# A four-layer graph network on one core: layer 0's sums in one PSUM bank, two quarters side by side, and paired loads of the adjacency matrix

## The chip, the cores and the metric

The kernel runs on one NeuronCore of a Trainium2 chip. The metric is the device time of one execution in microseconds; lower is better. A profile is one further execution, recorded by the hardware profiler, with a time of its own.

## The reference

There are 4096 nodes with 64 features each and a 4096 x 4096 matrix `adj` of zeros and ones, about 0.8% of them ones. Four layers follow each other, each of the form `x = x + layer(relu(layernorm(x)), adj)`. What matters here are the first two.

```python
# layer 0: each row of adj weighs its (up to 100) last neighbours by powers of 1/2
support = input @ weight
rank = jnp.cumsum(mask, axis=1)          # mask = adj != 0
deg = rank[:, -1:]
k = jnp.minimum(deg, 100.0)
pos = rank - (deg - k)
w = mask * jnp.where(pos > 0, 0.5 ** (k - pos), 0.0)
out = w @ support + bias
# layer 1: attention, masked by adj
att = sigmoid((2 + 2 * (qm @ k.T)) / att_scale + att_bias)
support = (adj * att) @ h
out = support / sqrt(abs(inner(support)))
```

Here `h`, `q` and `k` of layer 1 are linear maps of the features with a first component that is made from the others. Layer 2 applies a gated unit to `adj @ x` twice, and layer 3 a hyperbolic mean over `adj`.

## The kernel before

`adj` is held on the chip, transposed, as one byte per element: 64 tiles `A[q][i]` of 128 partitions x 2 x 1024. A *quarter* `q` is 1024 rows of the output, a *block* `b` is 128 neighbours, and a tile holds the two blocks `2i` and `2i+1`. The tiles stay for all four layers.

**Layer 0** (`stream0`, with `post0` behind it) takes the quarters one after another, and in each the 32 blocks from the last to the first. A block is loaded by POOL's queue, with a cast from f32 to bytes in the transfer, 512 KB from `in_adjT`; this load waits for the one eight loads back (`after=loads[-8:-7]`). One block in eight is *staged* instead: SP loads it as f32 into a working tile, POOL casts it (`L1210`), and VectorE tests its values (`test`). Then, for each half `c` of the quarter (512 rows), TensorE counts the ones that come later, with a triangular matrix (`ftri`), into a bank `cnt`; ACT or VectorE turns the counts into weights (`weigh`, `L1233` or `L1235`), reading the count's bytes; TensorE updates the counts with `fupd`, so that the next block can be counted. The weights of two rows share one f32 word, so an instruction of 256 words has 512 weights. Counting, weighing and updating are a loop: the next block of the same half can't be counted before this one has been weighed. `add` then multiplies the block's features `S0` by the weights: the weights are the stationary operand, eight matmuls of 128 x 128 a block, node-major, into two banks `sum`. `post0` reduces them, turns them by four transposes (`turn4`, `L1038`), multiplies by `w0` (`linear4`) and adds to `X[q]`.

**Between the layers** `pre1(q)` makes the keys `kT[q]`, the queries (sent through the DRAM tile `qs` to all partitions) and `S1[q]`. It is a chain of small instructions on VectorE, ACT, TensorE and POOL, whose `root` (`L997`) is a power on POOL, the engine that also issues the loads.

**Layer 1** (`stream1`) takes each quarter and in it pairs of blocks `i` from 0 to 15. For each half `c`, four f32 matmuls of 64 x 64 x 512 make the scores in two banks `sc`, ACT applies a sigmoid (`L1008`), VectorE multiplies by `A` (`L968`), and `add` sums into two banks `acc` with four matmuls of 64 x 64 x 512 for each block; `post1` adds the two banks. A *group* below is such a set of four matmuls: 128 for scores and 128 for sums. Pair `i` needs the keys of quarter `i // 4`.

**Order.** A planner (`Plan`) fixes the order of all engines when the kernel is built. It takes operations by priority and by the costs and limits written into it. Each engine then runs its own list in that order. PSUM has eight banks: places 0 to 3 can be taken in pairs, 4 to 7 are single. `limits` holds how many of a kind may be in use; `anywhere` names the kinds that may take any place; `single` lets at most three of the single banks be held by other kinds than `nw`. So two of `cnt` leave one of these for others.

The values of `adj` not tested in layer 0 are tested later by `later_test` (f32 loads on SP, `L1187` on VectorE, `L1189` and `L1190` on ACT), 36 of them spread over layer 1 and the rest after it. `general_kernel` is a second program for other inputs, which is not entered here.

Of the kernel before, what the change touches and what calls it, by code (L numbers as in the profile page):

```python
# [38 lines left out]
def general_kernel(ctx: ExitStack, tc: tile.TileContext, t: dict, out: bass.AP):  # L39
# [9 lines left out]

    nc = tc.nc  # L50
    adjT = t["adjT"]
    N = adjT.shape[0]
    NB = N // P
    HB = NB // NH
    HN = N // NH
# [161 lines left out]
    def aggregate(m, lhs, weigh, descending, evac, post):  # L217

        pairs = list(range(NB // 2))[::-1] if descending else list(range(NB // 2))
        packed = m == D
        for h in range(NH):
            n_acc = NCH // 2 if packed else NCH
            banks = [accp.tile([P, CW], F32, tag=f"acc{c}", name=f"acc{c}") for c in range(n_acc)]
            if packed:
                accs = [banks[c // 2][(c % 2) * D:(c % 2) * D + D, :] for c in range(NCH)]  # L230
            else:
                accs = [bank[:m, :] for bank in banks]

            def accumulate(i, pair, s, rhs):
                for j in ((1, 0) if descending else (0, 1)):
                    b = 2 * pair + j
                    for c in (2 * s, 2 * s + 1):
                        nc.tensor.matmul(accs[c], lhs(b), rhs(j, c),
                                         start=(i == 0 and j == int(descending)),
                                         stop=(i == NB // 2 - 1 and j == int(not descending)))  # L240

            behind = None
            for i, pair in enumerate(pairs):
                a = adjp.tile([P, 2, HN], F32, tag="a", name="a")
                nc.sync.dma_start(a, adjT[pair * 2 * P:(pair + 1) * 2 * P, h * HN:(h + 1) * HN]
                                  .rearrange("(j p) n -> p j n", p=P))
                for s in range(NCH // 2):
                    rhs = weigh(h, i, pair, s, a)
                    if behind is not None:
                        accumulate(*behind)  # L250
                    behind = (i, pair, s, rhs)
                if h > 0 and i == 1:
                    post(h - 1)
            accumulate(*behind)
            evac(h, accs)
        post(NH - 1)
# [377 lines left out]
class Plan:  # L634
# [61 lines left out]
    def find(self, b):  # L696
# [19 lines left out]
            return (best[1], best[2]) if best else (math.inf, None)  # L716
        if self.psn.get(b.kind, 0) + b.units > self.limits.get(b.kind, 8):
            return math.inf, None
        places = range(0, 4, 2) if b.units == 2 else range(8) if b.kind in self.anywhere else range(4, 8)
        if b.kind != "nw" and self.psn.get("single", 0) >= 3:  # L720
            places = [i for i in places if i < 4]
        best = None
# [178 lines left out]
def fast_kernel(ctx: ExitStack, tc: tile.TileContext, t: dict, out: bass.AP, flag: bass.AP):  # L901
    nc = tc.nc
    adjT = t["adjT"]
    N = adjT.shape[0]
    NB = N // P
    L = Layout()
    V, S_, G_ = nc.vector, nc.scalar, nc.gpsimd
# [5 lines left out]
    dram = ctx.enter_context(tc.tile_pool(name="fdram", bufs=1, space=bass.MemoryType.DRAM))  # L913

    plan = Plan(NSB, {"cnt": 2, "sum": 2, "sc": 4, "acc": 3, "acc2": 3, "acc3": 6, "nw": 4,
                      "w": (24, 16), "g": (5, 6), "stage": (5, 8), "qd": (4, 0), "mx": (4, 0)}, ("sum", "acc3"))

    sb_tiles = [const.tile([P, 2 * CW], F32, name=f"m{i}") for i in range(NSB)]
    st_tiles = [const.tile([P, 16], F32, name=f"s{i}") for i in range(NST)]
# [19 lines left out]
    def sb(units, name):  # L939
        return fresh("sb", units, name)  # L940
# [7 lines left out]
    def bank(kind, units=1):  # L948
        return fresh(kind, units, kind)
# [174 lines left out]
    def a8(q, b):  # L1124
        return A[q][b // 2].part(b % 2)[:, b % 2, :]
# [19 lines left out]

    S0 = {}

    loads = []

    def halves(dst, x, prio, relu=False):  # L1150

# [24 lines left out]

    def staged(q, b):
        n = q * NB + NB - 1 - b
        return n > 8 and n % 8 == 1

    def test(b, q, s, prio, cost):
        i = q * NB + b
# [9 lines left out]

    def later_test(b, q, after, cost):
        s = sb(4, "stage")
        dma(s, View(None, lambda: adjT[b * P:(b + 1) * P, q * 2 * CW:(q + 1) * 2 * CW]), P * 2 * CW * 5, 8.0, after=after)
        return test(b, q, s, 9.0, cost)


    def stream0(q, behind):
        cnt = [bank("cnt") for _ in range(2)]  # L1200
        sums = [bank("sum") for _ in range(2)]
        for b in range(NB)[::-1]:
            a = a8(q, b)
            src = View(None, lambda b=b: adjT[b * P:(b + 1) * P, q * 2 * CW:(q + 1) * 2 * CW])
            if b in behind:
                behind[b](loads[-1:], (q, b + 1))
            if staged(q, b):
                s = sb(4, "stage")
                dma(s, src, P * 2 * CW * 5, 1.0, after=loads[-2:-1])
                plan.op({"POOL": 1.4}, lambda e, a=a, s=s: G_.tensor_copy(a.get().bitcast(U8), s.get(), saturate=False),  # L1210
                        (s,), (a,), 1.0)
                test(b, q, s, 1.9, {"DVE": 1.58})
            else:
                loads.append(dma(a.bits(U8), src, P * 2 * CW * 4, 0.9 if len(loads) < 2 else 1.0, "POOL", after=loads[-8:-7]))
            wts = []
            for c in (0, 1):
                pairs = slice(c * CW // 2, (c + 1) * CW // 2)

                def count(e, c=c, a=a, pairs=pairs, b=b, wt=tri):
                    mm(cnt[c].get()[:, :CW // 2], wt, a.get().bitcast(F16)[:, pairs], False, b == 0)  # L1220

                if b == NB - 1:
                    plan.op({"PE": 0.12}, lambda e, c=c: mm(cnt[c].get()[:, :CW // 2], mean16, half16, True, False),
                            (triv,), (cnt[c],), 1.0, "full")
                plan.op({"PE": 0.112}, count, (a, triv), (cnt[c],), 1.0, "full")
                wt = sb(1, "w").bits(I16)
                wts.append(wt)

                def weigh(e, c=c, wt=wt):
                    o = wt.get().rearrange("p (n k) -> p n k", k=2)  # L1230
                    s = cnt[c].get()[:, :CW // 2].bitcast(I8).rearrange("p (n k) -> p n k", k=4)[:, :, :2]
                    if e == "ACT":
                        S_.activation(o, s, AF.Relu, scale=-128.0)  # L1233
                    else:
                        V.tensor_scalar(o, s, -128.0, 0.0, op0=ALU.mult, op1=ALU.max)  # L1235
                plan.op({"ACT": 0.6, "DVE": 0.69}, weigh, (cnt[c],), (wt,), 0.5)
                if b:
                    plan.op({"PE": 0.112}, lambda e, count=count: count(e, wt=upd), (a, triv), (cnt[c],), 1.0, "full")
            for c in (0, 1):
                def add(e, b=b, c=c, wt=wts[c]):  # L1240
                    s = S0[b // QB].get()[:, b % QB]
                    o = sums[c].get().rearrange("p (k n) -> p k n", k=4)
                    for d in range(4):
                        mm(o[:, d, :].rearrange("p (k d) -> p k d", d=D), wt.get()[:, d * P:(d + 1) * P].bitcast(BF16), s,
                           b == NB - 1 and d == 0, b == 0)
                plan.op({"PE": 0.24}, add, (wts[c], S0[b // QB]), (sums[c],), 2.0, "full")
        return sums

    def post0(q, sums, prio):
        g = nodes("agg")  # L1250
        for c in range(2):
            red(g.part(c)[:, c * CB:(c + 1) * CB, :], sums[c].re("p (b k d) -> p b d k", k=2, d=D), CW, prio)
        fm = sb(2, "aggT")
        copy(fm, turn4(flat(g), prio), prio=prio, scale=W0 / HALF)
        tt(X[q], X[q], blocks(linear4(fm, w("w0"), prio)), ALU.add, prio=prio)
        pre1(q, prio)

# [75 lines left out]

    ends = {}
    scores = []

    def stream1(q):
        qd = []
        for c in range(2):
# [3 lines left out]
                dma(v.part(r)[half, :], View(qS[q].buf, lambda c=c: qS[q].get()[c * D:(c + 1) * D, :]), D * CW * 4, 1.0,  # L1343
                    after=ends.get(("qd", q), ()))
            qd.append(v)
        acc = [bank("acc") for _ in range(2)]
        for i in range(NB // 2):
            gs = []
            for c in range(2):
# [16 lines left out]
            for j in range(2):  # L1366
                def add(e, i=i, j=j, gs=gs):
                    b = 2 * i + j
                    s = S1[b // QB].get()[:, b % QB, :]
                    for r in range(2):  # L1370
                        half = slice(r * D, (r + 1) * D)
                        for c in range(2):
                            mm(acc[r].get()[c * D:(c + 1) * D, :], s[half, :], gs[c].get()[half, j, :], b == 0, b == NB - 1)
                ends[1, q, i] = plan.op({"PE": 0.856}, add, (*gs, S1[(2 * i) // QB]), tuple(acc), 3.1, "corner")
        return acc

    def post1(q, acc, prio):
        a = sb(2, "a")
        fn(a, acc[0], AF.Copy, prio=prio)
        tt(a, a, acc[1], ALU.add, prio=prio)  # L1380
        sup = blocks(turn4(a, prio))
        sq = nodes("sq")
        square(sq, sup, prio=prio)
# [307 lines left out]
    def load_consts(after, behind):  # L1691
        gate(Wv, lambda: W[:1, :1], behind)
        dma(Wv, View(None, lambda: t["consts"][:, :L.at["scales"].stop]), P * L.at["scales"].stop * 4, 0.1, after=after)
        for q in range(NQ):
# [2 lines left out]
        subnormals(3.0)  # L1697

    load_x(3)
    behind = {NB - 2: lambda *a: load_x(2, *a), NB - 5: lambda *a: load_x(1, *a), NB - 9: lambda *a: load_x(0, *a),  # L1700
              NB - 13: load_consts}
    sums = {}
    for q in range(NQ):
        sums[q] = stream0(q, behind if q == 0 else {})
        post0(q, sums[q], 0.9 if q < NQ - 1 else 0.4)
    acc = {}
    for q in range(NQ):
        if q:
# [42 lines left out]
        for o in plan.order(NST):  # L1751
            o.emit(o.on)
    return plan


def pack_consts(given):

    import numpy as np
# [82 lines left out]
```

## Time and profile before

| what | value |
|---|---|
| median of three runs | 688.46 us (687.64 to 690.23) |
| profiled execution, own time | 691.17 us |
| profiled execution, span | 689.3 us |
| TensorE clock granted, mean | 0.976 |
| busy: TensorE, VectorE, ACT, POOL | 622.3, 548.6, 450.6, 167.9 us |
| first and last `ftri` matmul | 6.3 and 202.2 us |
| loads of `adj` on POOL | 113, issued from 1.2 to 182.1 us |
| loads of `adj` on SP | 128 (15 in layer 0) |

The span runs from the first instruction to the last; the execution's own time also has what lies around them. TensorE's busy time is an upper bound for the work that it had, since matmuls are pipelined and their ends are modelled. The stages of the span are layer 0 up to 203 us, layer 1 up to about 440, layer 2 up to about 600, layer 3 up to about 660, and an end without TensorE.

### The profile page before, as it was taken

The page shows a single profiled execution, that of the slowest core. Times are in us where ns is not written, and L with a number is a line of the kernel's source. Part 1 is how long each engine was busy: PE and PEld are TensorE (multiplying, and loading weights), DVE is VectorE, ACT ScalarE, POOL GpSimd, SP SyncE. Part 2 cuts the span into 40 slices and gives each one's busy share as a digit, 9 for nine tenths or more (in the row PEclk, how much of TensorE's full clock was granted, in tenths as well). Part 3 has the DMA queues.
Part 4 walks back from the last instruction along what each step waited for, and adds up shares of the span by engine and source line. Part 5 has one row for each costly group of instructions (what it writes and reads, how often), then busy time and mean ns, then how long its engine had stood idle before and what let it go on. Part 6 is the DMA issues. An engine that isn't in the chain of part 4 may idle for free.

```text
span 689.3 us, 14988 instructions
## 1 busy us (share of the span) xinstructions
PE 622.3 (90%) x6060; PEld 355.2 (52%) x6060; DVE 548.6 (80%) x1030; ACT 450.6 (65%) x680; POOL 167.9 (24%) x188
## 2 busy tenths in 40 slices
PE   4788889899999999999999999999999999999950
PEld 2666668678764443333333333344444444599950
DVE  5675776776768899998987799887988988985585
ACT  3464757577666666676665567645987698984463
POOL 6535564574422200200110010011000022202141
PEclk9899999999999999999999999999999999999995
DMA  9999989989902233422322231369689978420001
GB/s 99 181 251 106 95 66 147 178 73 157 125 17 62 77 93 97 120 62 93 108 57 97 92 112 62 123 220 390 202 264 352 342 250 260 154 63 2 3 31 36
DMA packets 39934, 91.64 MB, mean 133 GB/s; under 512 B 4656, under 2 KB 19632, under 8 KB 39856
## 3 DMA queue, kind: packets, MB, share of 16 engines
q1 hardware_dynamic: 23584, 75.78, 33.1%
q0 software_dynamic: 16272, 14.82, 24.2%
q8 instruction: 49, 0.80, 0.5%
q14 instruction: 29, 0.24, 0.1%
HBM read 130.82 MB, written 2.10 MB: 193 GB/s over the span
## 4 chain that ended last, share of the span: by engine, by line
PE 63%; DVE 16%; DMA 8%; ACT 6%; issue 3%; POOL 3%; SPq 0%; POOLq 0%; ACTq 0%; DVEq 0%
PE p L1029 61%; DVE m L968 4%; DMA A<-in_adjT 3%; ACT m L1008 3%; PE p L1038 3%; DMA m<-in_adjT 3%; DVE m L1235 2%; DVE m L985 2%; POOL s L997 2%; DMA m<-in_x_pm 2%; ACT m L1233 2%; DVE s L990 2%; DVE junk L1187 2%; POOL A L1025 1%; DVE s L968 1%
## 5 line engine op out<-in xcount | busy, mean ns | idle before, releaser
L1029 PE MATMUL p<-m,m 64*64 64x512 f32 (+1 forms) x3012 | 337.8, 476 | 8.5 <-ACT m L1008 3.7
L997 POOL TENSOR_TENSOR s<-s,powers 128x8 f32<-128x8 f32 (+1 forms) x45 | 89.3, 1992 | 461.4 <-DVE s L979 199.4
L1008 ACT ACTIVATE m<-p,fatt_add,fatt_mul 128x1024 f32<-128x1024 f32 x128 | 149.6, 1201 | 77.2 <-PE p L1029 63.6
L1029 PEld LDWEIGHTS <-m 128*128 128x128 bf16 (+1 forms) x2048 | 134.0, 105 | 75.5 <-issue 22.0
L968 DVE TENSOR_TENSOR m<-m,A 128x1024 f32<-128x1024 f32 x128 | 152.8, 1221 | 19.8 <-ACT m L1008 19.4
L1029 PEld LDWEIGHTS p<-m,m 64*64 64x64 f32 (+1 forms) x2040 | 81.0, 132 | 142.4 <-issue 81.8
L1233 ACT ACTIVATE m<-p 128x512 int16<-128x512 int8 x180 | 103.7, 596 | 52.5 <-PE p L1029 47.1
L1187 DVE SCALAR_TENSOR_TENSOR junk<-m 128x1024 uint8<-128x1024 f32 x98 | 119.5, 1220 | 8.2 <-DMA m<-in_adjT 7.3
L1029 PE MATMUL p<-A,m 128*64 128x512 fp8e4 x1024 | 116.4, 381 | 0.0
L1029 PE MATMUL p<-A,fupd 128*128 128x256 f16 x248 | 67.6, 283 | 13.9 <-DVE m L1235 6.0
L1235 DVE TENSOR_SCALAR m<-p 128x512 int16<-128x512 int8 x76 | 52.3, 690 | 30.7 <-PE p L1029 23.3
L1029 PE MATMUL p<-A,ftri 128*128 128x256 f16 x256 | 68.9, 286 | 6.5 <-POOL A L1210 3.8
L1008 ACT ACTIVATE m<-m 128x512 f32<-128x512 f32 (+4 forms) x96 | 53.6, 567 | 30.4 <-DVE m L968 14.6
L1025 POOL DMA_DIRECT2D A<-in_adjT x113 | 61.0, 553 | 39.7 <-DMA A<-in_adjT 38.4
L1029 PE MATMUL p<-m,A 128*128 128x132 f16 x1024 | 61.4, 220 | 1.5 <-ACT m L1008 1.2
L1029 PEld LDWEIGHTS <-A 128*128 128x128 fp8e4 x1024 | 60.1, 96 | 4.0 <-issue 4.0
L990 DVE TENSOR_REDUCE s<-m 128x8 f32<-128x512 f32 (+2 forms) x66 | 43.3, 661 | 9.1 <-DMA m<-in_x_pm 7.1
L1029 PEld LDWEIGHTS <-ftri 128*128 128x128 bf16 x256 | 25.6, 100 | 33.5 <-issue 26.1
L1008 ACT ACTIVATE m<-p 128x512 f32<-128x512 f32 (+4 forms) x40 | 19.2, 491 | 33.4 <-PE p L1029 24.0
L1190 ACT ACTIVATE junk<-m,big 128x1024 uint8<-128x1024 f32 x30 | 34.5, 1149 | 1.0
L1189 ACT ACTIVATE junk<-m 128x1024 uint8<-128x1024 f32 x30 | 31.4, 1047 | 1.7 <-DMA m<-in_adjT 1.5
L1038 PE MATMUL p<-fident,m 128*128 128x128 f32 x160 | 25.8, 284 | 6.8 <-DVE m L968 4.5
(102 smaller groups left out, 429.3 us busy)
## 6 DMA issues: line engine op xcount, KB each, us to landing
m<-in_adjT SPq DMA_DIRECT2D x128, 512.0 KB, 5.7
A<-in_adjT POOLq DMA_DIRECT2D x113, 128.0 KB, 9.9
m<-qs SPq DMA_DIRECT2D x16, 128.0 KB, 4.4
m<-m SPq DMA_DIRECT2D x16, 128.0 KB, 6.9
m<-in_x_pm SPq DMA_DIRECT2D x4, 256.0 KB, 6.6
qs<-m SPq DMA_DIRECT2D x4, 256.0 KB, 5.2
out_x<-m SPq DMA_DIRECT2D x3, 256.0 KB, 2.1
m<-in_consts SPq DMA_DIRECT2D x2, 256.0 KB, 5.2
```

The source lines that it names most:

```text
L968: return plan.op(cost or {"DVE": dve(n)}, lambda e: ENG[e].tensor_tensor(o.get(), a.get(), b.get(), op), (a, b), (o,), prio)
L990: return plan.op({"DVE": dve(n)}, lambda e: V.tensor_reduce(o.get(), a.get(), AX.X, ALU.add), (a,), (o,), prio)
L997: lambda e: G_.tensor_tensor(o.get(), a.get(), POWER[power].get().to_broadcast([P, n]), ALU.pow),
L1008: S_.activation(o.get(), a.get(), func, **k)
L1025: return plan.op({eng: 0.06 if eng == "SP" else 0.55}, lambda e: ENG[e].dma_start(o.get(), a.get()), (a,), (o,), prio, nbytes=nbytes, afte ...
L1029: nc.tensor.matmul(o, lhsT, rhs, start=start, stop=stop, skip_group_check=True)
L1038: nc.tensor.transpose(o[:, j * P:(j + 1) * P], s[:, j * P:(j + 1) * P], ident)
L1187: V.scalar_tensor_tensor(junk, s.get(), 0.0, s.get(), op0=ALU.not_equal, op1=ALU.not_equal, accum_out=odd[:, i:i + 1])
L1189: S_.activation(junk2, s.get(), AF.Exp, scale=-BIG0, accum_out=zeros[:, i:i + 1])
L1190: S_.activation(junk2, s.get(), AF.Exp, bias=big1, scale=BIG1, accum_out=ones_of[:, i:i + 1])
L1233: S_.activation(o, s, AF.Relu, scale=-128.0)
L1235: V.tensor_scalar(o, s, -128.0, 0.0, op0=ALU.mult, op1=ALU.max)
```

## The change

Five edits come together.

1. `adj` lies in DRAM by quarter, pair of blocks, partition, block of the pair and column, so that the two blocks of a tile are one run of 8 KB in each partition. POOL loads a tile at once (1 MB), except a quarter's first two blocks and the partner of a staged block. The waits are for the load six back, and for staged blocks four back.
2. Layer 0's sums take `S0` as the stationary operand, 64 wide, and the weights as the moving one, 512 wide: four matmuls a block, the two halves of the quarter on the two halves of the partitions of one bank. The result is feature-major, and `post0` loses its reductions and its transposes.
3. Quarters 1 and 2 are streamed together, block by block in turn. Each has one bank of counts with 512 words, so one weighing has 1024 weights. Quarters 0 and 3 keep two banks and weighings of 512. All counts are made in 64-wide matmuls.
4. Layer 1's first quarter sums in one bank, with two matmuls of 128 x 64 x 512 a block in place of four of 64 x 64 x 512.
5. `cnt` is put into places 0 and 1, and `sum` no longer into any place. Staged blocks fall on another residue of eight.

```diff
-        places = range(0, 4, 2) if b.units == 2 else range(8) if b.kind in self.anywhere else range(4, 8)
+        places = range(0, 4, 2) if b.units == 2 else range(2) if b.kind == "cnt" else range(8) if b.kind in self.anywhere else range(4, 8)
...
-                      ...}, ("sum", "acc3"))
+                      ...}, ("acc3",))
...
     def staged(q, b):
         n = q * NB + NB - 1 - b
-        return n > 8 and n % 8 == 1
+        return n > 8 and n % 8 == 5
...
-    def stream0(q, behind):
-        cnt = [bank("cnt") for _ in range(2)]
-        sums = [bank("sum") for _ in range(2)]
+    def stream0(qs, behind):
+        cnts = {q: [bank("cnt") for _ in range(2 // len(qs))] for q in qs}
+        sums_ = {q: bank("sum") for q in qs}
         for b in range(NB)[::-1]:
+            for q in qs:
+                block0(q, b, cnts[q], sums_[q], behind)
+        return sums_
+
+    def block0(q, b, cnt, sums, behind):
+        a = a8(q, b)
+        src = View(None, lambda: adjT[q, b // 2, :, b % 2, :])
...
+        if staged(q, b):
+            s = sb(4, "stage")
+            dma(s, src, P * 2 * CW * 5, 1.0, after=loads[-4:-3])
...
+        elif staged(q, b ^ 1) or b // 2 == NB // 2 - 1:
+            loads.append(dma(a.bits(U8), src, P * 2 * CW * 4.6, ..., "POOL", after=loads[-6:-5]))
+        elif b % 2:
+            loads.append(dma(A[q][b // 2].re("p j n -> p (j n)").bits(U8),
+                             View(None, lambda: adjT[q, b // 2].rearrange("p j n -> p (j n)")),
+                             2 * P * 2 * CW * 4.3, 1.0, "POOL", after=loads[-6:-5]))
...
+        parts = len(cnt)
+        wide = CW // parts
+        for c in range(parts):
+            def count(e, c=c, wt=tri):
+                s = a.get().bitcast(F16)
+                for h in (0, 1):
+                    half = slice(h * D, (h + 1) * D)
+                    if parts == 1:
+                        mm(cnt[c].get()[half, :], wt[:, half], s, False, b == 0)
+                    else:
+                        mm(cnt[c].get()[half, :wide]..., wt[:, half], s...[:, c], False, b == 0)
...
         def add(e):
+            for k in (0, 1):
+                for c in (0, 1):
+                    mm(sums.get()[c * D:(c + 1) * D, :].rearrange("p (j n) -> p j n", n=P), s[:, k, :], v[c],
+                       b == NB - 1 and k == 0, b == 0 and k == 1)
+        plan.op({"PE": 0.432}, add, (*wts, S0[b // QB]), (sums,), 2.0, "narrow")
 
     def post0(q, sums, prio):
-        g = nodes("agg")
-        for c in range(2):
-            red(g.part(c)[:, c * CB:(c + 1) * CB, :], sums[c].re("p (b k d) -> p b d k", k=2, d=D), CW, prio)
         fm = sb(2, "aggT")
-        copy(fm, turn4(flat(g), prio), prio=prio, scale=W0 / HALF)
+        copy(fm, sums, prio=prio, scale=W0 / HALF)
...
+    EARLY = 1
+    GROUPS = ((0,), (1, 2), (3,))
     def stream1(q):
...
-        acc = [bank("acc") for _ in range(2)]
+        early = q < EARLY
+        acc = [bank("acc") for _ in range(1 if early else 2)]
...
                     s = S1[b // QB].get()[:, b % QB, :]
+                    if early:
+                        for c in range(2):
+                            mm(acc[0].get()[c * D:(c + 1) * D, :], s, gs[c].get()[:, j, :], b == 0, b == NB - 1)
+                        return
...
-    for q in range(NQ):
-        sums[q] = stream0(q, behind if q == 0 else {})
-        post0(q, sums[q], 0.9 if q < NQ - 1 else 0.4)
+    for qs in GROUPS:
+        sums = stream0(qs, behind)
+        for q in qs:
+            post0(q, sums[q], 0.9 if q < NQ - 1 else 0.4)
...
-        "x": given("x"), "adjT": transposed("adj"),
+        "x": given("x"), "adjT": given("adj").reshape(NQ, 2 * CW, -1, 2, P).transpose(0, 2, 4, 3, 1),
```

## Prediction

> **What bounds the kernel now.** I read the page's slices first, then busy time by stretches, then the chain of waits, then the groups by form.
>
> ```profile
> PE   4788889899999999999999999999999999999950
> ...
> DMA  9999989989902233422322231369689978420001
> ```
>
> Columns are 17.2 us. TensorE is busy nearly everywhere, but up to about 185 us the DMA engines are full too. Layer 0 and layer 1 have different limits.
>
> ```profile
> 6.00:61.00 55.00, 41.28 (x368) 32.26 (x368) 33.51 (x63) 28.72 (x52) 27.79 (x40) 0.91 1.09 176
> ...
> 158.00:203.00 45.00, 41.95 (x445) 34.28 (x442) 32.19 (x61) 32.09 (x59) 18.48 (x22) 1.00 0.78 108
> ...
> 300.00:360.00 60.00, 60.00 (x544) 20.17 (x536) 53.44 (x65) 38.91 (x37) 5.09 (x2) 1.00 0.25 76
> ```
>
> The stretches of 6 to 203 us are the quarters of layer 0: the first `ftri` matmul starts at 6.3, the last at 202.2 (the tile view of `ftri`). From 300 to 360 TensorE has no gap, and 544 records (two per f32 matmul, four matmuls a group) are 68 groups: **0.88 us a group**. Layer 1 is bound by TensorE. Layer 0 is paced by three things close together, as the chain and the queue of POOL show.
>
> ```profile
> 86.21 3.64 POOL A L1025 x7
> 89.84 6.19 issue
> 96.07 3.86 POOL s L997 x2
> ...
> 197.66 1.04 PE p L1029 x12
> 198.72 1.04 PE p L1029 x12
> ```
>
> ```profile
> 54.07 0.53 POOL L1025 DMA_DIRECT2D A<-in_adjT  x1 [0.79 <-DMA A<-in_adjT]
> 55.29 0.53 POOL L1025 DMA_DIRECT2D A<-in_adjT  x1 [0.70 <-DMA A<-in_adjT]
> 56.50 0.53 POOL L1025 DMA_DIRECT2D A<-in_adjT  x1 [0.69 <-DMA A<-in_adjT]
> 57.76 0.53 POOL L1025 DMA_DIRECT2D A<-in_adjT  x1 [0.73 <-DMA A<-in_adjT]
> ```
>
> The second is POOL's timeline. When POOL only loads, it waits for the load eight back and issues one each 1.24 us: 512 KB of `adj` read in 1.24 us is 423 GB/s. **All 128 blocks at that pace are 159 us**, `x` and the constants (1.5 MB) 3.6 us more, the first landing 5 us: a DMA floor of 168 us. The last load is issued at 182.1 and takes some 9 us, so it lands near 191. The 23 us above the floor are holes, of which the chain shows one: seven loads, then POOL stands for 6.2 us before two roots of `pre1`, then works 3.9 us, and issues nothing for 10 us, as long as eight loads in flight last. The stream itself ends 11 us after the last landing. And where blocks come back to back, a block is 12 matmuls in **1.04 us** of TensorE.
>
> **What the Trainium skill says.** "DMA: Bandwidth & Descriptors", Rules for kernel authors, wants 1 MiB or more per DMA; its section Anatomy of one DMA gives 2.0 us plus bytes over 436 GB/s. The trace's 423 GB/s with eight loads of 512 KB in flight is within 3% of that, so size alone can buy little. "TensorEngine Tiling (Array Packing)", Key Properties: column tiles run in parallel, and a change of mode drains TensorE. The layer 2 row below agrees on the first; no row prices the drain. "VectorE: DVE Perf Modes", The TRN2 errata, prices a read of PSUM by ScalarE at 172 + n cycles of 1.2 GHz and by VectorE at 120 + n of 0.96 GHz: 0.57 and 0.66 us for n = 512, where the trace has 0.596 and 0.690.
>
> **The change, part by part.** Prices:
>
> ```profile
> L1029 PE MATMUL p<-A,m 128*64 128x512 fp8e4 x1024 | 116.4, 381 | 0.0
> L1233 ACT ACTIVATE m<-p 128x512 int16<-128x512 int8 x180 | 103.7, 596 | 52.5 <-PE p L1029 47.1 <-DVE m L1235 2.1 <-issue 0.5
> ...
> L1029 PEld LDWEIGHTS <-m 128*64 128x64 f16 x1024 | 55.4, 110 | 62.7 <-issue 16.3
> L1235 DVE TENSOR_SCALAR m<-p 128x512 int16<-128x512 int8 x76 | 52.3, 690 | 30.7 <-PE p L1029 23.3 <-ACT m L1233 6.7
> ```
>
> *TensorE in layer 0.* A narrow 512-wide matmul of two side by side costs 116.4/1024 = 0.114 us, its weight load (55.4/1024 = 0.054) hidden. The sums become 4 of these, 0.455 us a block, for 8 of 128 x 128. Counts become 8 narrow of 256 in quarters 0 and 3, 4 narrow of 512 in quarters 1 and 2; by streamed columns both are 0.455. No row shows a 256-wide narrow one. Bounds for a block: 0.91 with all loads hidden; with every count's load exposed, 0.91 + 8 x 0.054 = 1.34 (quarters 0 and 3) and 1.13 (1 and 2). I take 0.95, because layer 3's 128-wide loads and 132-wide matmuls run 1024 in 61.4 us, 0.06 each, so loads hide behind matmuls of similar length. Then 128 x (1.04 - 0.95) = 11.5 us of TensorE fall away. The built order has 18 of layer 1's 256 groups ahead of layer 0's last matmul; now it is 3 (24 records in the window to 202.5), because `single` lets three of the four single banks be held at once: 2 for `cnt` leave 1, and `acc` asks for 2. With `cnt` in banks 0 and 1, sums (2) and one `acc` fit. These 15 cost 15 x 0.88 = 13.2 us inside layer 0, about what is freed there. **After layer 0 they are 13 us less.**
>
> *Weighing and posts.* 64 instructions of 1024 replace 128 of 512. With the page's slope on the measured rows (an estimate) they take 1.02 on ACT and 1.22 on DVE: some 128 x 0.62 - 64 x 1.1 = 9 us less over both, with a longer link of the loop count, weigh, update, but two quarters advance per link. At 0.25 + 1.1 + 0.25 and hops of 0.3 a link is some 1.9 to 2.3 us for two blocks, under the 2.48 that their loads take. `post0` loses 8 reductions (5.5 us of DVE) and 4 turns (2.6 us by 25.8/160 a transpose); only quarter 3's share, 2 x 0.69 + 4 x 0.16, about 2 us, leads a chain that is waited for. The first `post1` loses one 0.69 add, under cover of layer 1. I count these at nothing; without cover they give 2 us.
>
> *Loads.* 45 pair loads and 23 single ones replace 113, so POOL issues 45 times less, 25 us at 0.55, which are mostly waits now. Six may fly, on average 10 blocks (113/68 each) for 8: 12.4 us against 10. Thus a stop like that at 89.8 is covered by 2.5 us more. A pair is available when its second half lands: up to 1.24 us later, which matters for the first pair only, since later blocks lead by 10 us. Behind a waiting load on POOL stand the casts of staged blocks and the roots of `pre1`, whose DVE steps wait for them; these are as many as before. SP has the same 15 staged loads, let go by the load four back; two tests of layer 1 slip into layer 0, 2.5 us of DMA. 8 KB rows for 4 KB: the trace has none; no gain up to 3% of 159 us, or a loss of as much, 5 us both ways. I take no change of rate, and that **two thirds to three quarters of the 34 us between the floor and 202 stay**: holes go from 23 to 13, the lag at the end from 11 to 3. Layer 0 ends at 184, 18 us sooner.
>
> *What is late next.* Quarters 1 and 2 end together, so `pre1` of quarter 1 starts 32 blocks later, and only key blocks 0 to 3 (16 groups, and two scores more) can go ahead. After layer 0 the next wait is for quarter 3's keys: now they come at 238 (`qs` issued at 238.2), 35 us after layer 0, with 30 groups, 26 us, and pre-ops between. The new order has 30 there too, so that cover holds. Everything from layer 2 on has the same order.
>
> *Sum.* The profiled execution's own time is 691.2 (span 689.3); the median of the runs is 688.5, 2.7 lower. 691.2 - 18 - 13.2 = 660.0 for a profile, **657 as a median**.
>
> **Rivals.**
> - *The loads gain nothing.* POOL still stops at roots, the DMA queue has the same holes. Then layer 0 ends at 202 and 13 us remain: 675. For it: POOL waited 44.8 us for DVE in layer 0; against: more blocks in flight.
> - *The floor is reached.* Last landing at 168, end at 171: 31 + 13 us, 644. Against it: three roots of `pre1` for each of two quarters now fall together.
> - *Narrow weight loads are exposed (slower).* Each matmul of the counts has its own 64-wide load, 64 x 8 + 64 x 4 = 768 of them. At the upper bound a block is 1.24 on average: 158 us for 133 now, plus 29 for the rest (transposes, `W` products, presets, groups) and 13 for the new groups: 200. With half of the present 202 - 133 - 29 = 40 us of waits layer 0 ends at 220: 18 later, 13 back, 693. It decides once the exposed loads eat the 31 us of the forecast, 0.04 us for each of 768, three quarters of a load. Against it are the layer 2 and 3 rows; for it, that none of them is 256 wide and that `pre1` and scores change the mode in between.
> - *No difference:* the 15 groups lengthen layer 0 by what they save later, with the loads unchanged: 688.
>
> **Chances.** Forecast 0.52, floor 0.15, loads gain nothing 0.17, exposed loads 0.11, no difference 0.05. So faster by over 0.5% (3.4 us, about what a measurement of this kernel tells from no change) 0.84, within it 0.05, slower 0.11. The range goes from the floor, 643, to 686, which leaves out the slower case and little else; the forecast alone is 649 to 668.
>
> **What would show it.** Right: last narrow count matmul of layer 0 at 176 to 192, 18 layer 1 groups before it, POOL's pair loads 2.5 us apart where it only loads, then 0.88 us a group with TensorE full up to layer 2. A block of 12 or 8 matmuls back to back in 0.95 us. Wrong: pairs further apart than 2.6 us; 1.2 us or more for a block; or TensorE idle some 10 us before the scores of quarter 3's keys, which would mean that the groups moved were the cover of `pre1`.

## The result, and the profile after

The changed kernel is slower. Its median is **773.97 us** (771.04 to 777.09, four runs) against 689.35 us for the kernel before beside it: a ratio of 1.123, 95% interval 1.1176 to 1.1284. The profiled execution took 773.04 us, its span is 771.2 us. One execution each of e1 and e21 below ran much longer at a lower granted clock, and their medians leave it out.

Three lines of the slices on the changed kernel's page, a column now 19.3 us; the second is the granted TensorE clock in tenths:

```profile
PE   4656667685777778999999999999999999999950
...
PEclk9766699789999979999999999999999999999995
DMA  9998054899706402131322322424977997720000
```

TensorE is not full before the seventeenth column, and the DMA engines have long stretches with little or nothing. Four stretches of the changed kernel follow; the prediction shows three of the same windows of the kernel before (columns: start and end, length, busy time of TensorE, weight loads, VectorE, ACT, POOL, then clock, DMA share and GB/s):

```profile
6.00:61.00 55.00, 33.31 (x244) 19.85 (x244) 26.46 (x49) 19.77 (x35) 21.28 (x28) 0.77 1.07 172
61.00:158.00 97.00, 65.86 (x439) 36.84 (x437) 40.28 (x70) 35.96 (x48) 20.38 (x26) 0.80 0.54 54
158.00:203.00 45.00, 33.72 (x238) 13.77 (x236) 19.95 (x18) 20.42 (x20) 10.79 (x17) 0.99 0.96 152
300.00:360.00 60.00, 58.98 (x388) 19.54 (x388) 52.14 (x76) 37.46 (x40) 9.36 (x5) 1.00 0.25 78
```

In the first of these, 55 us long, TensorE begins 244 matmuls where it began 368, and no compute engine is full; the DMA engines still are (1.07), and fall to 0.54 in the second. The last row is layer 1, nearly as full as before. The tile view of `ftri` puts the end of layer 0 at **296.8 us** (202.2 before): 94.6 us later. What follows takes 771.2 - 296.8 = 474.4 us, where it took 689.3 - 202.2 = 487.1: 12.7 us less. So the loss lies in layer 0 alone.

The chain of waits of the changed kernel, in quarter 0 (start, duration, what), shows how a block goes:

```profile
83.06 0.61 ACT m L1257
83.66 0.02 issue
83.69 0.70 DVE m L1259
84.39 0.04 issue
84.43 1.07 PE p L1029 x12
85.50 0.02 issue
85.53 0.61 ACT m L1257
86.13 0.02 issue
86.16 0.70 DVE m L1259
86.86 0.04 issue
86.90 1.08 PE p L1029 x8
```

One block takes from 84.43 to 86.90, 2.47 us, and the two weighings in it, on two engines and of two different banks, never overlap: VectorE starts 0.03 us after ACT ends. In the chain of before, two blocks start 1.06 us apart (197.66 and 198.72). The waits say the same. First the kernel before, then the changed kernel (engine and line, what it waited for, total us, times, longest), each over its layer 0:

```profile
DVE m L1235 <- ACT m L1233: 6.7, 8, 1.2
...
PE p L1029 <- DVE m L1235: 6.0, 11, 2.0
...
PE p L1029 <- ACT m L1233: 4.1, 10, 0.6
```

```profile
DVE m L1259 <- ACT m L1257: 56.8, 35, 3.9
...
PE p L1029 <- DVE m L1259: 42.9, 45, 2.0
PE p L1029 <- ACT m L1257: 40.8, 62, 1.2
```

A weighing on VectorE that waits for one on ACT has no reason in the arithmetic: they read different counts and write different weights. At 85.50 TensorE has made both counts of the block (the last four of its twelve matmuls are `ftri`, two for each half); VectorE, which only reads its own half, still waits for ACT, which only reads the other. These are waits on semaphores: in the trace the instruction of VectorE at 86.16 waits on the semaphore that ACT's instructions raise, and on none of TensorE's.

**Theory.** Edit 5 put the two `cnt` into places 0 and 1, which are the two halves of one two-bank PSUM tile, `p0`. Instructions of different engines on that tile are put in order, whichever half they touch, so the two loops of a block become one. Before, each `cnt` had a tile of one bank. **Rivals:** narrow weight loads that don't hide; the lower clock; the queues of POOL and SP with pair loads; the order of quarters 1 and 2.

### The profile page after: what moved, and what is told of

Its sections match the earlier page's. It is cut to its first block, busy times and chain, and to the rows that moved or that the text cites. A ratio compares the mean times of both kernels' runs of the same rounds, so it can differ in the third digit from the quotient of the medians.

```text
span 771.2 us, 14016 instructions
## 1 busy us (share of the span) xinstructions
PE 644.4 (84%) x5664; PEld 320.1 (42%) x5664; DVE 539.0 (70%) x1004; ACT 444.3 (58%) x633; POOL 139.8 (18%) x143
## 4 chain that ended last, share of the span: by engine, by line
PE 61%; DVE 15%; ACT 13%; DMA 6%; issue 3%; POOL 1%; ACTq 0%; SPq 0%; POOLq 0%; DVEq 0%
PE p L1029 59%; ACT m L1257 9%; DVE m L1259 6%; DVE m L968 4%; ACT m L1008 2%; PE p L1038 2%; DMA m<-in_adjT 2%; DVE junk L1187 2%; DVE m L985 1%; DMA m<-in_x_pm 1%; POOL s L997 1%; DVE s L990 1%; DMA qs<-m 1%; DMA m<-qs 1%; DMA A<-in_adjT 1%
## 5 line engine op out<-in xcount | busy, mean ns | idle before, releaser
L1029 PE MATMUL p<-m,m 64*64 64x512 f32 (+2 forms) x2420 | 334.8, 565 | 5.7 <-DVE m L1718 3.2
L1257 ACT ACTIVATE m<-p 128x512 int16<-128x512 int8 (+1 forms) x130 | 94.8, 734 | 148.2 <-PE p L1029 140.4
L1029 PEld LDWEIGHTS p<-m,m 64*64 64x64 f32 (+1 forms) x1952 | 76.1, 132 | 150.7 <-issue 87.6
L1259 DVE TENSOR_SCALAR m<-p 128x512 int16<-128x512 int8 (+1 forms) x62 | 54.6, 880 | 113.0 <-ACT m L1257 56.8
L1029 PEld LDWEIGHTS <-m 128*64 128x64 f16 x1536 | 93.5, 115 | 77.3 <-issue 18.2
L1029 PE MATMUL p<-A,fupd 128*64 128x256 f16 (+1 forms) x372 | 64.0, 357 | 67.7 <-DVE m L1259 38.3
L1029 PEld LDWEIGHTS <-fupd 128*64 128x64 bf16 x372 | 35.4, 121 | 120.3 <-issue 115.2
L1029 PE MATMUL p<-A,ftri 128*64 128x256 f16 (+1 forms) x384 | 67.3, 356 | 18.0 <-ACT m L1257 12.3
L1029 PEld LDWEIGHTS <-ftri 128*64 128x64 bf16 x384 | 30.4, 122 | 30.6 <-issue 24.3
L1025 POOL DMA_DIRECT2D A<-in_adjT x68 | 37.0, 555 | 8.9 <-DMA A<-in_adjT 8.1
L1008 ACT ACTIVATE m<-p 128x512 f32<-128x512 f32 (+4 forms) x40 | 19.2, 491 | 32.7 <-PE p L1029 24.6
```

Source lines behind the costliest of these rows:

```text
L1008: S_.activation(o.get(), a.get(), func, **k)
L1025: return plan.op({eng: 0.06 if eng == "SP" else 0.55}, lambda e: ENG[e].dma_start(o.get(), a.get()), (a,), (o,), prio, nbytes=nbytes, afte ...
L1029: nc.tensor.matmul(o, lhsT, rhs, start=start, stop=stop, skip_group_check=True)
```

## The experiments

All in one table. "Rest" is the profiled span less the start of the last `ftri`; e2 and e3 have one run, the others a median of three or more, and the kernel before beside them was 689.0 to 690.1 us.

| kernel | us | last `ftri` | rest |
|---|---|---|---|
| before | 689.35 | 202.2 | 487.1 |
| changed | 773.97 | 296.8 | 474.4 |
| e1_cnt_singles | 699.24 | 207.9 | 490.3 |
| e2_before_cnt_p0 | 822.43 | 335.7 | 484.9 |
| e3_cnt_two_tiles | 696.80 | 204.0 | 491.0 |
| e4_quarters_in_turn | 708.39 | 215.8 | 491.1 |
| e5_single_loads | 693.62 | 200.2 | 491.2 |
| e6_no_staged_12 | 693.23 | 196.8 | 493.7 |
| e7_full_counts | 709.46 | 216.9 | 490.2 |
| e12_own_tiles | 698.95 | 208.4 | 488.2 |
| e13_own_tiles_single_loads | 680.07 | 200.4 | 479.2 |
| e14_own_tiles_no_staged_12 | 679.38 | 192.9 | 482.2 |
| e15_pairs_no_staged_12 | 690.40 | 210.6 | 476.7 |
| e20_staged_window_2 | 682.36 | 204.7 | 475.3 |
| e21_staged_window_3 | 696.51 | 213.6 | 480.5 |
| e22_staged_residue_1 | 694.84 | 207.8 | 484.8 |

### Is it the shared tile?

**e1_cnt_singles**, the changed kernel with

```diff
-        places = ... else range(2) if b.kind == "cnt" else range(8) if b.kind in self.anywhere ...
+        places = ... else range(8) if b.kind in self.anywhere ...
...
-                      ...}, ("acc3",))
+                      ...}, ("sum", "acc3"))
```

> The changed kernel with the place rule of before: `cnt` in the single banks again and `sum` anywhere; all else as changed. In the built order the weighs on DVE that wait for PE alone rise from 4 of 62 to 26 of 59, and no scores of layer 1 go ahead of layer 0's end. Theory (shared tile: with both `cnt` in one two-bank tile the two loops of a block wait for each other): the 94.6 us of layer 0 come back, its last ftri starts at 175 to 205 instead of 296.8, and with some 487 us after it as in before the time is 665 to 695. Rivals (narrow weight loads exposed; lower granted clock; POOL held by roots and pair loads; order of quarters 1 and 2): none of them is touched, layer 0 still ends near 297 and the time is 770 to 785.

Measured: 699.24 us, a ratio of 1.0128 to before (1.006 to 1.0196); layer 0 ends at 207.9. Of the 94.6 us of layer 0, 88.9 are gone. Both numbers miss the theory's ranges by 3 to 5 us, and no rival came near.

**e2_before_cnt_p0**, the kernel before with the same rule put in:

```diff
-        places = ... else range(8) if b.kind in self.anywhere ...
+        places = ... else range(2) if b.kind == "cnt" else range(8) if b.kind in self.anywhere ...
...
-                      ...}, ("sum", "acc3"))
+                      ...}, ("acc3",))
```

> The kernel before with one thing of the change: `cnt` in places 0 and 1 (both halves of the two-bank tile p0), `sum` in the single banks. Loads, 128-wide counts and sums, order of quarters all as before. Theory (shared tile): the loop of the two halves becomes one, count, weigh on ACT 0.60, weigh on DVE 0.69, update, with hops some 2.0 to 2.5 us a block for the 1.04 to 1.5 of before: the last ftri starts at 260 to 320 and the time is 745 to 810. Rivals: nothing they blame is in this kernel, so 685 to 695.

Measured: 822.43 us in one run, more than the range; layer 0 ends at 335.7, so a block takes (335.7 - 6.4) / 128 = 2.57 us on average, and the rest, 484.9 us, is about as long as in the kernel before. Its chain of waits:

```profile
297.23 0.60 ACT m L1233
297.83 0.04 issue
297.88 0.39 PE p L1029 x2
...
298.35 0.60 ACT m L1233
298.95 0.04 issue
299.00 0.61 PE p L1029 x6
```

Here both halves go weigh, count, weigh, count in one line. None of the rivals is in this kernel: wide weights, single loads, quarters in turn. The rule alone costs 132 us. Its part on `sum` is not what costs: e3, next, keeps that part.

**e3_cnt_two_tiles**, the changed kernel with one digit different:

```diff
-        places = ... else range(2) if b.kind == "cnt" else ...
+        places = ... else (0, 2) if b.kind == "cnt" else ...
```

> The changed kernel with one number different: `cnt` in places 0 and 2 instead of 0 and 1, thus the first halves of the two two-bank tiles p0 and p1. Scores of layer 1 find no pair of banks while layer 0 lasts, so none go ahead. Theory (shared tile): the weighs of the two halves no longer wait for each other, the last ftri starts at 175 to 205, the time is 665 to 695. If what costs is a bank of a two-bank tile as such, or anything of the rivals (narrow loads, clock, POOL, order of quarters): near 297 and 770 to 785.

Measured: 696.8 us in one run, 2 above the range; layer 0 ends at 204.0, in it. Two halves of two different two-bank tiles don't hinder each other. The timeline of this kernel in quarters 1 and 2 shows the two weighings of 1024 side by side (start, duration, engine, in brackets the idle time before):

```profile
128.93 1.02 ACT L1257 ACTIVATE m<-p 128x1024 int16<-128x1024 int8 x1 [2.74 <-PE p L1029]
129.22 1.23 DVE L1259 TENSOR_SCALAR m<-p 128x1024 int16<-128x1024 int8 x1 [0.58 <-PE p L1029]
```

Both wait for TensorE alone. The clock rival falls here too: the mean granted clock is 0.97 from 6 to 205 us, and 0.75 from 6 to 338 us in e2, where the rule alone was put in. So the 0.77 and 0.80 of the changed kernel went with the serial loop and not the other way. What e1 to e3 show is that the shared tile makes the order, through semaphore waits that stand in the program; why the tile is followed as a whole, and whether the two banks could have been read at once, they don't show.

### Are narrow counts dear, is the order of quarters?

**e4_quarters_in_turn**, e3 with

```diff
-    GROUPS = ((0,), (1, 2), (3,))
+    GROUPS = ((0,), (1,), (2,), (3,))
```

> The kernel e3_cnt_two_tiles (the change with `cnt` in places 0 and 2: 696.8 us, last ftri at 204.0) with the quarters one after the other again: GROUPS of one quarter each, all counts in two banks of 256 words. In e3 quarters 1 and 2 take 61 to 157 us, 96 us for the 88 of before, and POOL stands 17.1 us before the first root of their pre1 at 160.9. Theory A (what still keeps the gain away is the order side by side: pre1 of quarters 1 and 2 fall together after both, and a root holds POOL's queue): layer 0 ends 8 to 18 us earlier, 678 to 690. Theory B (it is the staged loads behind `qs` on SP's queue, or the pair loads): these stay, 693 to 700.

Measured: 708.39 us. Theory A falls: in turn, layer 0 is 11.8 us longer, not shorter. Whether the order side by side is what helps stays open; orders set by other edits differ by as much (below).

**e7_full_counts**, e4 with 128-wide counts:

```diff
-                for h in (0, 1):
-                    mm(cnt[c].get()[half, :wide]..., wt[:, half], ...)
+                mm(cnt[c].get()[:, :wide]..., wt, ...)
```

> e4_quarters_in_turn with the counts as before: 128-wide weights, two 256-wide matmuls per `ftri` and per `fupd` instead of four 64-wide ones (512 per quarter-pair fewer loads, 1007 narrow matmuls become 503). Sums stay 64-wide. Rival of the prediction (narrow counts pay for exposed weight loads, 0.04 to 0.054 us for each of some 1000 loads, 40 to 54 us of TensorE, half of it on the path): faster than e4 by 10 to 30 us. Shared tile theory with no exposed loads: within 4 us of e4; slower if anything[...].

Measured: 709.46 us; its ratio to before and that of e4 are both 1.0275. **Narrow counts cost nothing that can be measured here, and bring nothing.** The timeline of e3 shows no exposed weight loads. Between starts lie 0.11 us for two 256-wide narrow counts side by side and 0.43 for the four sums:

```profile
171.57 0.30 PE L1029 MATMUL p<-A,ftri 128*64 128x256 f16 x2
171.68 0.62 PE L1029 MATMUL p<-m,m 128*64 128x512 bf16 x4
172.11 0.30 PE L1029 MATMUL p<-A,fupd 128*64 128x256 f16 x2
```

A block is 4 x 0.11 + 0.43 = 0.87 us of TensorE.

### Loads and staged blocks

**e5_single_loads**, e3 with the loads of before:

```diff
-            dma(s, src, P * 2 * CW * 5, 1.0, after=loads[-4:-3])
+            dma(s, src, P * 2 * CW * 5, 1.0, after=loads[-2:-1])
...
-        elif staged(q, b ^ 1) or b // 2 == NB // 2 - 1:
-            loads.append(... a.bits(U8) ... "POOL", after=loads[-6:-5]))
-        elif b % 2:
-            loads.append(... A[q][b // 2] ... "POOL", after=loads[-6:-5]))
+        else:
+            loads.append(... a.bits(U8) ... "POOL", after=loads[-8:-7]))
```

> e3_cnt_two_tiles (696.8 us) with the loads of before: each block of `adj` its own 512 KB load of 4 KB runs, let go by the load eight back, staged ones by the load two back. Theory A (order of quarters): no change beyond 3 us, 693 to 700. Theory B1 (pair loads and the staged window of four do harm, by letting staged loads onto SP late or early against `qs`): 5 to 12 us back, 684 to 692. Theory B2 (pair loads helped, more blocks in flight): slower, 700 to 708.

Measured: 693.62 us, 3.2 under a single run of e3: by itself it doesn't decide between A and B1.

**e6_no_staged_12**, e3 with

```diff
-        return n > 8 and n % 8 == 5
+        return n > 8 and n % 8 == 5 and q in (0, 3)
```

> e3_cnt_two_tiles (696.8 us) with no staged blocks in quarters 1 and 2: POOL loads all of them, and their tests move to layer 1 (8 of 15). In e3 the staged loads stand in SP's queue behind `qs` of quarter 0 and its reading back (99.8 to 109.9 us), the first lands at 123.3, POOL waits 19.0 us for it, and TensorE has no counts from 115.3 to 124.4. Theory B (SP's queue): that hole closes, layer 0 ends some 6 to 10 us sooner, 686 to 692 with up to 3 us lost to the tests. Theory A (order of quarters alone): unchanged or a little slower by the tests, 695 to 702.

Measured: 693.23 us, 1.2 above theory B's range. Layer 0 ends 7.2 us sooner, and the rest, to which the tests moved, is 2.7 us longer. The hole of theory B is real. In e3's chain of waits it reads

```profile
99.84 7.51 DMA qs<-m
...
109.94 13.35 DMA m<-in_adjT
123.34 1.05 POOL A L1215
```

`qs` of quarter 0 is written, SP waits 7.5 us for it before it reads it back, and the staged load behind that on SP's queue is issued only then; POOL, in order too, stands for its cast, and all loads behind with it.

### All of the change, with a tile for each count

**e12_own_tiles** cuts the tiles anew and leaves all else of the change; the planner's tests for single places follow the new numbers:

```diff
-        places = range(0, 4, 2) if b.units == 2 else range(2) if b.kind == "cnt" else ... else range(4, 8)
+        places = ((2, 4) if b.units == 2 else (0, 1) if b.kind == "cnt" else (4, 5) if b.kind == "sum" else
+                  range(8) if b.kind in self.anywhere else (0, 1, 6, 7))
...
-    ps_tiles = [psp.tile([P, (2 if i < 2 else 1) * CW], ...
+    ps_tiles = [psp.tile([P, (2 if i in (2, 3) else 1) * CW], ...
```

> The change as it stands, with only the PSUM tiles cut anew: places 0, 1, 6 and 7 are single tiles, 2-3 and 4-5 the two-bank tiles; `cnt` in 0 and 1, `sum` in 4 and 5, scores in 2-3 and later 4-5. Every buffer finds a bank when it does in the change, so groups of layer 1 go ahead again (e3_cnt_two_tiles had none), but the two `cnt` have a tile each. Shared tile theory: last ftri at 198 to 210 (204.0 in e3, the groups partly in TensorE's idle time), and after it 472 to 478 us as in the change (474.4), not the 491.0 of e3: 672 to 688. If groups ahead lengthen layer 0 by what they save: 692 to 698. If a shared tile was not the cause: 770.

Measured: 698.95 us, ratio 1.0137 (1.0117 to 1.0158). So **75 of the 84.6 us go with the shared tile**: layer 0 ends 88.4 us sooner, and the rest is 13.8 us longer; it was expected at 472 to 478 and is 488.2. An obvious rival is that the planner merely set another order. The traces rule it out for most of layer 0: in the changed kernel and in e12, TensorE's first 1086 matmuls, VectorE's first 178 instructions, ACT's 123 and POOL's 90 are the same in the same order (by operation, tiles without buffer numbers, and shape). The last of these matmuls starts at 230.7 us in the changed kernel and at 166.8 us in e12. So 64 us fall away with the order unchanged, and only behind that do the orders part.

**e13_own_tiles_single_loads** is e12 with e5's edit, **e14_own_tiles_no_staged_12** is e13 with e6's.

> e12_own_tiles with the single loads of before (e5's edit). In e5 they gave 3 us against e3 (693.6 to 696.8). If pair loads and the window of four are what lets staged loads come late: 2 to 6 us under e12. If they only shifted holes: within 2 us of e12.

> e13_own_tiles_single_loads with no staged blocks in quarters 1 and 2 (e6's edit, which gave 3.6 us against e3, with the last ftri 7.2 us sooner and 2.7 us more after layer 0 for the tests moved there). If the two edits take away the same hole (the staged load behind `qs`): within 2 us of e13. If they take away different ones: 2 to 4 us under e13.

Measured: 680.07 us, ratio **0.9856** (0.9825 to 0.9888), and 679.38 us, 0.9861 (0.9836 to 0.9885). Both beat both kernels. e13 lies 18.9 us under e12, three times the top of what was expected. In e14's profile layer 0 ends 7.5 us sooner and the rest is 3.0 longer; of the 4.5 us that this leaves the medians show 0.7, which is within their spread.

**e15_pairs_no_staged_12** is e12 with e6's edit; **e20_staged_window_2** and **e21_staged_window_3** are e12 with `after=loads[-2:-1]` and `after=loads[-3:-2]` for `after=loads[-4:-3]` at the staged load; **e22_staged_residue_1** is e12 with `n % 8 == 1`.

> e12_own_tiles (699.0 us, pair loads) with no staged blocks in quarters 1 and 2, their tests in layer 1; so it differs from e14_own_tiles_no_staged_12 (679.4) in the pair loads alone. POOL stood 18.2 and 8.9 us for staged loads in e12, with the stream out of blocks. If those waits are what made e12 19 us slower than e13, and pair loads by themselves cost nothing: 677 to 685. If pair loads themselves keep blocks away (six in flight, a pair there only when its second half has landed, POOL stopped by roots): 688 to 697.

> e12_own_tiles (699.0 us) with one number different: a staged load is let go by the load two back, as before, instead of four back. If the window of four puts the staged loads behind `qs` and its reading back on SP's queue, and their casts early in POOL's: 680 to 690. If any window does that with pair loads, since the planner reckons `qs` and its reading back at some 5 us where the trace has 9.8: 694 to 702.

> e12_own_tiles (699.0 us; staged loads let go by the load four back) with that number at three; at two (e20_staged_window_2) it was 682.4. In e20 POOL's longest wait for a staged load was no shorter (19.8 us, 18.2 in e12) and 12.9 of the 16.6 us lie after layer 0. If the window matters by how long POOL waits for staged blocks, three lies between: 687 to 695. If the window only makes the planner set another order, most of all after layer 0: anything from 678 to 700 with no relation to the number, and layer 0 within 5 us of 208.4.

> e12_own_tiles with the staged blocks of before (n % 8 == 1 instead of 5), as many, four blocks later in each eight. If the change's residue is what costs e12 its 9 us against the kernel before: 680 to 690. If only the planner's order moves: anything from 678 to 700, with the difference to e12 after layer 0 at least as much as in it.

Measured: 690.40, 682.36, 696.51 and 694.84 us. A window of two, three and four gives 682, 697 and 699: a step between two and three, and no grading. Nor is it POOL's wait. Its waits up to 205 us, in e12 and then in e20:

```profile
POOL A L1216 <- DMA m<-in_adjT: 31.5, 6, 18.2
POOL s L998 <- DVE s L980: 31.3, 6, 13.9
POOL s L998 <- DVE m L978: 21.2, 3, 8.8
```

```profile
POOL A L1216 <- DMA m<-in_adjT: 40.5, 6, 19.8
POOL s L998 <- DVE m L978: 25.2, 5, 10.1
POOL s L998 <- DVE s L980: 20.4, 6, 7.6
```

The faster kernel waits longer for staged blocks. By their own ranges, e15 fits pair loads that keep blocks away and e20 a harmful window of four; e21 is outside the range of a graded window, and its layer 0 lies 5.2 us from that of e12, just over the 5 allowed to a mere change of order; e22 fits such a change (0.6 us in layer 0, 3.4 after it).

Of the 16.6 us between the spans of e12 and e20, 3.7 lie before the last `ftri` and 12.9 after it. After it TensorE is busy for nearly as long in both (445.1 us in e12, 443.4 in e20), so 11.2 of the 12.9 us are time in which it stands. The edit does make the planner set another order: from TensorE's 159th matmul on the two lists differ, also behind layer 0, where the length moved between 474.4 and 488.2 us over the changed kernel and e12 to e22, with nearly the same work. That the order is the cause, and which part of it, was not shown.

One difference does repeat. In each pair of kernels with pair loads and with single loads, layer 0 ends sooner with single ones: by 3.8 us (e3 and e5), 8.0 (e12 and e13), 4.3 (e20 and e13, with the same window for staged loads) and 17.7 (e15 and e14). POOL's waits for staged loads up to the last `ftri` fall with it, from 24.6 us to 7.8, from 31.5 and 40.5 to 8.4, and from 9.5 to 1.6. So pair loads lengthen layer 0 in every form tried here; how much of that comes through these waits the runs don't separate.

## Why the prediction was wrong, point by point

- **The failed step: the loop of count, weigh and update.** The prediction gave each `cnt` of edit 5 a bank and thought of two loops that run beside each other: 0.95 us a block back to back, 1.9 to 2.3 for a link of two blocks in quarters 1 and 2. It asked for how many banks are free, and not which tile they belong to. The runs showed one loop with both halves in it, 2.47 us a block in the changed kernel and 2.57 in e2. Times 128, 2.47 is 316 us; layer 0 ended at 296.8, since quarters 1 and 2, where one weighing has 1024 weights, take less: 2.07 us a block from their first to their last count (89.8 to 222.5). The rival on the slower side was another mechanism (exposed weight loads); e7 shows it absent.
- **TensorE's price for a block**, 0.95: 0.87 measured in e3. Right in kind; the bounds upwards were not needed. But the sign that the prediction asked for, blocks back to back in 0.95 us, did not come even with the tiles apart: the closest blocks of e3 start 1.1 us apart, where before they started 1.06 apart. There ACT weighs both halves without a pause, 0.57 us each (its timeline in quarter 3), so in this stretch the time taken off TensorE had no effect on the pace:

```profile
186.57 2.83 ACT L1257 ACTIVATE m<-p 128x512 int16<-128x512 int8 x5
```

- **Weighing**: a 1024-wide one at 1.02 us on ACT and 1.22 on VectorE; the changed kernel has 1.023 and 1.224. Here the estimate from the Trainium skill, "VectorE: DVE Perf Modes", The TRN2 errata, held.
- **The groups ahead**, 13.2 us: 12.7 less after layer 0, with 17 of the 18 groups ahead. TensorE's busy time after layer 0 fell from 453.3 us to 441.4, so the step was right as work moved. Kernels with at most three groups ahead (e1, e3 to e7) have a rest of 490.2 to 493.7 us, the changed one and e12 to e22, with 7 to 17 ahead, 474.4 to 488.2. That the rest shortens by as much was in part luck: e12 has 15 groups ahead and TensorE's busy time down to 445.1, and its rest is 1.1 us longer than before.
- **The link in quarters 1 and 2** once the tiles are apart: in e3 ACT weighs at 128.93, 131.36 and 134.00, so 2.4 to 2.6 us for two blocks. The term of 1.9 to 2.3 was too low, and the link is as long as the loads' 2.48.
- **Layer 0 shorter by 18 us: this failed too**, though the shared tile hides it. With the tiles apart it ends between 192.9 and 216.9. The prediction's own sentence does not agree with itself here: of 34 us it lets 13 + 3 = 16 stay, which is less than half, and calls it two thirds to three quarters. The holes were to fall from 23 us to 13. The stretch of layer 0 as a whole, first before, then e3:

```profile
6.00:203.00 197.00, 168.80 (x1686) 135.87 (x1685) 138.12 (x254) 123.65 (x222) 103.30 (x137) 0.97 0.98 128
```

```profile
6.00:205.00 199.00, 157.63 (x1392) 93.87 (x1395) 120.87 (x221) 113.77 (x172) 74.22 (x92) 0.97 0.90 126
```

  Where POOL only loads, the DMA share of a 20 us stretch is about 1.09 before and 1.07 in e3. At that rate (an estimate) the transfers are 197 x 0.98 / 1.09 = 177 us and 199 x 0.90 / 1.07 = 167 us: pair loads need less, but the holes went from 20 to 32 us. That more blocks in flight cover POOL's stops was the wrong half. The prediction left the staged casts out, as no more than before; POOL stands for them 24.6 us in e3 by its waits, where it stood 2.1 before, with loads behind them. First the kernel before, then e3:

```profile
POOL A L1210 <- DMA m<-in_adjT: 2.1, 2, 1.6
```

```profile
POOL A L1215 <- DMA m<-in_adjT: 24.6, 5, 19.0
```

- **The pace of pair loads**, 2.5 us apart: e3 issues two at 139.26 and 141.71, 2.45 apart. Right.
- **POOL** in the changed kernel stood once for 43.7 us before a root, with the DMA engines empty (its timeline):

```profile
57.79 0.53 POOL L1025 DMA_DIRECT2D A<-in_adjT  x1 [0.63 <-DMA A<-in_adjT]
102.02 1.66 POOL L997 TENSOR_TENSOR s<-s,powers 128x8 f32<-128x8 f32 x1 [43.70 <-DVE s L979]
```

  This looks like a cause of its own; in e12, where POOL's list is the same up to there, the same root waits 8.73 us. So it follows from the late end of quarter 0: `pre1` comes late, and its roots stand in POOL's queue ahead of loads.

## What to carry to other kernels

A free PSUM bank is not a free buffer: ask which tile it is cut from, and whether two loops that should run beside each other meet in one. When instructions on two engines abut to within some hundredths of a microsecond and read different data, look for what they share before looking at prices. And where a planner sets the order, an edit to one window can move the time by over two per cent (e12 and e20: 16.6 us): measure each part of a change alone, and take a difference of that size for a cause only when a second edit of the same kind repeats it.

## What the runs showed of the hardware that was not expected

- The Trainium skill, "Perfetto Trace Analysis", Matmuls, says that independent matmul groups should rotate through different PSUM banks, so that the evacuation of one overlaps the matmuls of the next. In the changed kernel and e2 the counts did lie in different banks, and their weighings did not overlap; in e3 they lie in different tiles, and do (128.93 and 129.22 above). A bank of a two-bank tile is no hindrance as such: places 0 and 2 of e3 are a bank each of two such tiles. The order came from semaphores in the program, so it shows how this kernel is built; what the two banks themselves allow was not tested.
- The Trainium skill, "TensorE: Matmul & The Clock Gate", Part 1: The HAM clock gate, has the clock fall after an idle window of about 3.4 us; further on in the same part it names short idles between groups of matmuls as a second way. In the serial loop it is the short ones. TensorE's gaps there are about 1.4 us (it ends at 85.50 and begins at 86.90); from 61 to 158 us the longest is 2.0, TensorE is 68% busy by the table of stretches, and its mean granted clock is 0.80. In e2 the longest from 6 to 338 us is 1.7, and the clock there is 0.75. That the lower clock lengthens the serial loop in turn is likely and was not tested: a 256-wide narrow count took 330 ns on average in the changed kernel, 285 in e3.
